# Half a batch of the last residual moved from transposes to GpSimd adds by channel, and the loads split by step

## The chip, the cores and the metric

One NeuronCore of a Trainium2 chip runs the whole program. The metric is device time in microseconds of one execution; lower is better. Engines are named as the profile names them: PE is TensorE, DVE is VectorE, ACT is ScalarE, POOL is GpSimd, SP is the engine whose queue issues nearly all DMAs.

## The reference

The input `x` has 4 batches of 128 channels and 64 × 64 positions, float32. Per batch three things follow each other:

```python
# layer 0: attention over all 4096 positions, 64 media channels, no mask
out = x + wo @ (softmax(k^T q) v)
# layer 1: LayerNorm per position, causal attention, 128 channels
t = t + attn(ln_t(t))
# feed-forward: LayerNorm, W, BatchNorm over all positions of all batches, then a recurrence
def step(yt, wx_t):
    yt = jax.nn.sigmoid(wx_t + yt @ Vt)
    return (yt, yt)
y0 = zeros;  _, ys = jax.lax.scan(step, y0, swapaxes(Wx, 0, 1))
t = t + swapaxes(ys, 0, 1)
```

The scan runs over 4096 positions of each batch. The result is returned by channel.

## The kernel before

`fast_path` does the work; `general_path` is a plain second form behind a branch, taken only if a flag says that the fast one's assumptions did not hold. It did not run in the profiled execution.

**Attention.** For each batch b come the blocks of layer 0 and then those of layer 1, in the order g = 1, 0, 2, ..., 7 (a block is 512 positions). A loop over slots issues scores, exponentials, sums and products; what follows a block is a chain of small steps, each pushed into a list with a due slot (`push`, `yield n, step`), at most one step of each layer being run in a slot. The chain of a block of layer 1 is `finish1`: `first` (line 886 on) divides and adds the residual into `xs`, and for batches from `BY_C` = 2 on stores the block by token into the DRAM tile `x2t` (line 898, four DMAs); `norm` and `second` prepare the input of the feed-forward; for the batches below `BY_C` a step `kept` (line 925) brings the block to channels first with one DVE transpose (`squares`, line 758) and stores it into the DRAM tile `x2c` (line 765, four DMAs); `third` writes the feed-forward's product W·x over the block in `xs`.

**Recurrence.** The scan is cut into `NCH` = 256 chunks of `STEPS` = 16 positions per batch. All chunks run side by side: each is warmed up for `WARM` = 6 steps on the positions before it, and then takes its 16 steps. So a step of one batch is one product of 128 × 256 columns. `step(b, s)`: PE multiplies the states by `vf` into `ps_y` (line 1317), DVE adds the scaled input (`z`, line 1328), ACT applies the sigmoid (line 1332). A round s runs the four batches, then `residual(s - 1)`, then `add(s)`. From s = 1 on the orders on PE, DVE, ACT, POOL and SP are pinned (`pin`) as written.

**Output.** Batches 0 and 1 leave by channel: `add(s)` adds the states of step s and `xc` (512 columns, line 1339) on GpSimd and stores the sum (line 1341). `sums` has three buffers. Batches 2 and 3 leave by token: `residual(s)` transposes four tiles of 128 × 128 states on PE (line 1348) into `ps_r`, DVE adds them to `xr` in place (line 1352), and SP stores that (line 1353).

**Loads.** `xc` (two DMAs of 2 MB from `x2c`, line 1272) and then `xr` (four of 1 MB from `x2t`, line 1277) are issued on SP in that order just behind the last stores of line 898. After the rounds the kernel compares end states with start states (`difference`, `away`, lines 1375 to 1389), forms the flag (line 1414), and all engines load it and branch.

Of the kernel before, what the change touches and what calls it, by code (L numbers as in the profile page):

```python
# [15 lines left out]
P = 128  # L16
# [5 lines left out]
BY_C = 2  # L22
# [4 lines left out]
def general_path(  # L27
# [12 lines left out]
    f_gamma: bass.AP,  # L40
    f_beta: bass.AP,
    out_c: bass.AP,
    out_t: bass.AP,
):
    nc = tc.nc
# [241 lines left out]
    with tc.tile_pool(name="wx", bufs=1) as wxp, tc.tile_pool(name="fwork", bufs=3) as wk:  # L287
        wx = wxp.tile([P, N, B], F32, name="wx")
        stats = wxp.tile([P, B * NB, nc.vector.BN_STATS_DIM], F32, name="stats")
        with tc.tile_pool(name="ps_ln", bufs=2, space=PSUM) as ps_ln, tc.tile_pool(  # L290
            name="ps_wx", bufs=3, space=PSUM
        ) as ps_wx:
            for b in range(B):

                def project(blk, xhat, b=b):
                    wp = ps_wx.tile([P, BLK], F32, tag="w", name="wx_ps")
                    nc.tensor.matmul(wp, lhsT=wf, rhs=xhat, start=True, stop=True)
                    nc.vector.bn_stats(stats[:, b * NB + blk, :], wp)
                    nc.scalar.copy(wx[:, ts(blk, BLK), b], wp)

                layernorm(b, ps_ln, wk, project)


        mv = wxp.tile([P, nc.vector.BN_AGGR_DIM], F32, name="mv")
        nc.vector.bn_aggr(mv, stats)
        scale = wxp.tile([P, 1], F32, name="scale")
        nc.vector.tensor_scalar(scale, mv[:, 1:2], BN_EPS, None, ALU.add)
        nc.vector.reciprocal(scale, scale)
        nc.scalar.activation(scale, scale, AF.Sqrt)
        nc.vector.tensor_tensor(scale, scale, gamma, ALU.mult)  # L310
        shift = wxp.tile([P, 1], F32, name="shift")
        nc.vector.tensor_tensor(shift, mv[:, 0:1], scale, ALU.mult)
        nc.vector.tensor_tensor(shift, beta, shift, ALU.subtract)

        STEPS = BLK // B
        with tc.tile_pool(name="ys", bufs=3) as ysp, tc.tile_pool(
            name="ps_y", bufs=2, space=PSUM
        ) as ps_y, tc.tile_pool(name="ps_o", bufs=2, space=PSUM) as ps_o:

            def preload(kb):  # L320
                wn = wk.tile([P, STEPS, B], F32, tag="wn", name="wn")
                nc.vector.tensor_scalar(wn, wx[:, ts(kb, STEPS), :], scale, shift, ALU.mult, ALU.add)
                ps = ps_y.tile([P, STEPS, B], F32, tag="y", name="y_ps")
                nc.tensor.matmul(ps, lhsT=ident, rhs=wn, start=True, stop=False, skip_group_check=True)
                return ps

            nblk = N // STEPS
            prev = None
            nxt = preload(0)
            for kb in range(nblk):  # L330
                ps = nxt
                y = ysp.tile([P, STEPS, B], F32, tag="y", name="y")
                for t in range(STEPS):
                    if prev is not None:
                        nc.tensor.matmul(
                            ps[:, t, :], lhsT=vf, rhs=prev, start=False, stop=t == STEPS - 1, skip_group_check=True
                        )
                    nc.scalar.activation(y[:, t, :], ps[:, t, :], AF.Sigmoid)
                    prev = y[:, t, :]
                    if t == STEPS // 2 and kb + 1 < nblk:  # L340
                        nxt = preload(kb + 1)
                o = ysp.tile([P, B, STEPS], F32, tag="o", name="o")
                nc.gpsimd.tensor_tensor(o, xs[:, :, ts(kb, STEPS)], y.rearrange("p t b -> p b t"), ALU.add)

                S = out_c.shape[2]
                K = STEPS // S
                g, j = kb // TPB, kb % TPB
                for b in range(BY_C):
                    oc = ysp.tile([P, S, K], F32, tag="oc", name="oc")
                    nc.vector.tensor_copy(oc, o[:, b].rearrange("p (k s) -> p s k", s=S))  # L350
                    for q in range(TPB):
                        nc.sync.dma_start(out=out_c[b, :, :, ds(((g * TPB + q) * TPB + j) * 2, 2)], in_=oc[:, :, ts(q, 2)])
                op = ps_o.tile([P, B - BY_C, P], F32, tag="o", name="oT_ps")
                for b in range(BY_C, B):
                    nc.tensor.transpose(op[:, b - BY_C, :], o[:, b, :], ident)
                oT = ysp.tile([P, B - BY_C, P], F32, tag="oT", name="oT")
                nc.vector.tensor_copy(oT, op)
                R = STEPS // TPB
                for q in range(TPB):
                    nc.sync.dma_start(  # L360
                        out=out_t[:, ds(((g * TPB + q) * TPB + j) * R, R), :].rearrange("b n c -> n b c"), in_=oT[ts(q, R)]
                    )

# [1 line left out]
def fast_path(  # L367
# [13 lines left out]
    f_gamma: bass.AP,  # L381
    f_beta: bass.AP,
    out_c: bass.AP,
    out_t: bass.AP,
    flag: bass.AP,
):
# [25 lines left out]
    xs = xpool.tile([P, B, N], F32, name="xs")  # L412


    x2c = dram.tile([BY_C, P, N], F32, name="x2c")
    x2t = dram.tile([B - BY_C, N, P], F32, name="x2t")

    joint = const.tile([P, 2 * B, P], F32, name="joint")
    slots = iter(range(2 * B))
# [97 lines left out]
    with tc.tile_pool(name="batch", bufs=1) as batch, tc.tile_pool(name="rows", bufs=2) as rowp, tc.tile_pool(  # L517
# [363 lines left out]
        def finish1(b, g, turn):  # L881
# [4 lines left out]
            def first():  # L886
                denominators(1, b, g, mem["own"])
                joined(1, b, g, mem["op"] if turn else projected1(agg, final))
                if final:
                    early_product(1, *WHOLE[0])  # L890
                    early_sigmoid(1, *WHOLE[0])
                    for part in WHOLE[1:]:
                        early_step(1, part)
                    early_step(2, WHOLE[0])
                if b >= BY_C:
                    to = x2t[b - BY_C, ts(g, BLK)].rearrange("(q j t) c -> q t j c", q=Q, j=TPB)
                    for q in range(Q):
                        nc.sync.dma_start(out=to[q], in_=xs[ts(q, S), b, ts(g, BLK)].rearrange("p (j c) -> p j c", c=P))
                mem["xh"] = wk.tile([P, TPB, P], F32, tag="xh2", name="xh2")
                mem["of"] = moments(b, g)  # L900
                if final:
                    in_range(True)
# [4 lines left out]
            def second():  # L907
# [10 lines left out]
                    return  # L918


                by_c = dram2.tile([P, BLK], F32, tag="by_c", name="by_c")
                stored(mem["xh"], by_c)
                nc.sync.dma_start(out=mem["xhT"], in_=by_c)

            def kept():

                stored(xs[:, b, ts(g, BLK)].rearrange("p (j c) -> p j c", c=P), x2c[b, :, ts(g, BLK)])

            def third():

# [46 lines left out]
            if not final:  # L977
                yield 1, norm
            yield 2, second
            if b < BY_C:  # L980
                yield 1, kept
            if turn:
                late.append(third)
# [278 lines left out]
    with tc.tile_pool(name="xr", bufs=1) as xrp, tc.tile_pool(name="y", bufs=2) as yp, tc.tile_pool(  # L1262
# [3 lines left out]
    ) as ps_r, tc.tile_pool(name="ps_m2", bufs=1, space=PSUM) as ps_m2, tc.tile_pool(name="ps_y", bufs=1, space=PSUM) as ps_y:  # L1266

        HALVES = NCH // P
        by_chunk = lambda t: t.rearrange("b n c -> (b n) c").rearrange("(m q s) c -> s q m c", q=P, s=STEPS)
        xc = xrp.tile([P, BY_C, NCH, STEPS], F32, name="xc")  # L1270
        for b in range(BY_C):
            pin(nc.sync.dma_start(out=xc[:, b].rearrange("p k s -> p (k s)"), in_=x2c[b]))
        xr = xrp.tile([P, B - BY_C, HALVES, STEPS, P], F32, name="xr")
        for b in range(B - BY_C):
            for h in range(HALVES):
                pin(
                    nc.sync.dma_start(
                        out=xr[:, b, h], in_=x2t[b].rearrange("(h q s) c -> h q s c", q=P, s=STEPS)[h]
                    )
                )  # L1280

        mv = xrp.tile([P, nc.vector.BN_AGGR_DIM], F32, name="mv")
        nc.vector.bn_aggr(mv, ends)
# [50 lines left out]

        def add(s):

            t = sums.tile([P, BY_C, NCH], F32, tag="sum", name="sum")
            by_grid = lambda t: t.rearrange("p b (g c) -> p b g c", c=CPB)
            ins = nc.gpsimd.tensor_tensor(by_grid(t), by_step[:, :BY_C, s], by_grid(xc[:, :, :, s]), ALU.add)
            tc.keep_in_program_order(ins)  # L1340
            tc.keep_in_program_order(nc.sync.dma_start(out=out_c[:, :, s].rearrange("b c k -> c b k"), in_=t))


        def residual(s):

            ps = ps_r.tile([P, TPB, P], F32, tag="r", name="yT_ps")
            for j in range(TPB):
                ins = nc.tensor.transpose(ps[:, j], states(BY_C + j // HALVES, s)[:, j % HALVES], ident)
                if not j:
                    pin(ins)  # L1350
            t = xr.rearrange("p b h s c -> p (b h) s c")[:, :, s]
            pin(nc.vector.tensor_tensor(t, t, ps, ALU.add))  # L1352
            pin(nc.sync.dma_start(out=by_chunk(out_t)[s], in_=t))

        met = ps_m2.tile([P, BY_C, NCH], F32, name="met")
        gap = xrp.tile([P, B], F32, name="gap")
# [124 lines left out]
```

## Time and profile before

| what | us |
|---|---|
| median of three runs (2014.79 to 2014.90) | 2014.89 |
| the profiled execution | 2014.68 |
| its span, first to last instruction | 2012.9 |
| last scores of the attention start | 1941.96 |
| first `x2c` load issued (line 1272) | 1951.62 |
| first step of the recurrence with the final scale (line 1328) | 1957.87 |
| first `add` on GpSimd (line 1339) | 1971.67 |
| first matmul of the comparison (line 1375) | 2005.44 |
| flag written (line 1414) | 2009.16 |

Some 1950 us are attention, and some 50 us the recurrence; the rest is the end. In the page a busy share is over the whole span, so the engines of the last 55 us have to be looked at by themselves. DMA issues of the page that matter here:

```profile
x2c<-sqT SPq DMA_DIRECT2D x64, 64.0 KB, 1.8
x2t<-xs SPq DMA_DIRECT2D x64, 64.0 KB, 1.8
...
xc<-x2c SPq DMA_DIRECT2D x2, 2048.0 KB, 10.1
xr<-x2t SPq DMA_DIRECT2D x4, 1024.0 KB, 17.4
out_x<-sum SPq DMA_DIRECT2D x16, 256.0 KB, 2.2
out_x<-xr SPq DMA_DIRECT2D x16, 256.0 KB, 2.3
```

The last column is the median time in us from the issue to the landing. A start with a duration in a timeline merges neighbouring instructions of one kind ("x4"); what stands in brackets is the idle time of the engine ahead of it and what ended it.

### The profile page before, as it was taken

How to read it: one execution, taken by the hardware profiler on the slowest of the kernel's cores; microseconds unless marked ns; L12 is line 12 of the kernel's file. 1: busy time of each engine (PE TensorE's matmuls, PEld its weight loads, DVE VectorE, ACT ScalarE, POOL GpSimd, SP SyncE). 2: the span in 40 equal slices, each digit the busy share in tenths (PEclk: the TensorE clock that was granted, in tenths of full speed). 3: DMA queues.
4: the chain of work that ended last, by engine and by line, in shares of the span. 5: the costliest groups of instructions: out<-in, count | busy, mean ns of one | idle time of the engine just before them, and what ended most of it. 6: DMA issues, size and time to landing. Idle time of an engine off the chain costs nothing.

```text
span 2012.9 us, 31340 instructions
## 1 busy us (share of the span) xinstructions
PE 2003.2 (100%) x11896; PEld 875.4 (43%) x11896; DVE 1456.0 (72%) x2816; ACT 974.7 (48%) x1053; POOL 140.3 (7%) x241
## 2 busy tenths in 40 slices
PE   9999999999999999999999999999999999999998
PEld 3333354444333345444433334444433333544457
DVE  4799877545789987555589997654478998764568
ACT  5666633332666653333466664333356665333247
POOL 1000011000000001000000001000000000110014
PEclk9999999999999999999999999999999999999999
DMA  3111112210110111320111111231010111120027
GB/s 106 44 34 23 22 33 59 63 43 16 43 54 14 22 23 40 72 69 16 43 34 47 23 23 28 53 79 37 16 43 2 23 22 23 32 53 17 16 99 257
DMA packets 218603, 89.02 MB, mean 44 GB/s; under 512 B 142176, under 2 KB 203360, under 8 KB 217680
## 3 DMA queue, kind: packets, MB, share of 16 engines
q1 hardware_dynamic: 217728, 86.43, 17.4%
q8 instruction: 94, 1.54, 0.3%
q14 instruction: 61, 0.50, 0.1%
q0 software_dynamic: 288, 0.39, 0.1%
q10 hardware_dynamic: 432, 0.16, 0.0%
HBM read 45.84 MB, written 36.89 MB: 41 GB/s over the span
## 4 chain that ended last, share of the span: by engine, by line
PE 96%; DVE 2%; DMA 1%; ACT 0%; issue 0%; SPq 0%; POOL 0%; DVEq 0%; ACTq 0%; POOLq 0%
PE s_ps L1034 23%; PE acc L1094 22%; PE acc L1083 22%; PE s_ps L1019 22%; PE o_ps L688 1%; PE r_ps L639 1%; PE wx_ps L956 1%; PE kr_ps L576 1%; DVE z L1328 1%; DMA xr<-x2t 1%; PE v_ps L588 1%; PE o_ps L700 1%; DVE xr L1352 0%; ACT p L1028 0%; PE warm_ps L533 0%
## 5 line engine op out<-in xcount | busy, mean ns | idle before, releaser
L1063 DVE TENSOR_TENSOR dsum<-dsum,p 128x1024 f32<-128x1024 f32 x692 | 845.3, 1222 | 402.5 <-ACT p L1037 295.7
L1028 ACT ACTIVATE p<-s_ps,nshift 128x1024 f32<-128x1024 f32 x512 | 570.0, 1117 | 312.6 <-PE s_ps L1019 286.8
L1037 ACT ACTIVATE p<-s_ps 128x1024 f32<-128x1024 f32 (+2 forms) x288 | 274.5, 953 | 601.8 <-PE s_ps L1034 580.0
L1083 PE MATMUL acc<-p,v 64*64 64x512 f32 x4096 | 527.9, 589 | 0.0
L1019 PE MATMUL s_ps<-kr,swap 64*64 64x512 f32 x2048 | 522.6, 590 | 1.3 <-ACT p L1028 1.3
L1019 PE MATMUL s_ps<-kr 64*64 64x512 f32 x2048 | 522.6, 590 | 0.0
L1034 PE MATMUL s_ps<-rows,xhT 128*128 128x512 f32 (+3 forms) x1152 | 500.7, 558 | 0.0
L1094 PE MATMUL acc<-p,xh 128*128 128x512 f32 (+3 forms) x1152 | 500.2, 557 | 0.0
L1034 PEld LDWEIGHTS s_ps<-rows,xhT 128*128 128x128 f32 x1152 | 215.0, 190 | 244.7 <-issue 202.7
L1094 PEld LDWEIGHTS acc<-p,xh 128*128 128x128 f32 x1152 | 216.1, 190 | 239.8 <-issue 223.4
L1083 PEld LDWEIGHTS acc<-p,v 64*64 64x64 f32 x4096 | 156.6, 133 | 282.9 <-issue 274.3
L1019 PEld LDWEIGHTS s_ps<-kr,swap 64*64 64x64 f32 x2048 | 141.7, 133 | 144.6 <-issue 135.7
L1019 PEld LDWEIGHTS s_ps<-kr 64*64 64x64 f32 x2048 | 141.7, 133 | 134.6 <-issue 133.1
L728 POOL TENSOR_TENSOR ln_rstd<-ln_var,mhalf 128x4 f32<-128x4 f32 x64 | 69.9, 1093 | 1185.5 <-DVE ln_var L726 1185.4
L1071 DVE TENSOR_TENSOR dsum<-dsum,p 128x256 f32<-128x256 f32 (+1 forms) x120 | 56.0, 499 | 59.8 <-POOL p L1043 59.8
L714 DVE SCALAR_TENSOR_TENSOR xs<-o_ps,recs,xs 128x128 f32<-128x128 f32 x256 | 70.5, 343 | 5.4 <-PE o_ps L700 1.7
L744 DVE TENSOR_SCALAR xh<-xs,ln_mv,ln_rstd 128x128 f32<-128x128 f32 x252 | 70.1, 341 | 1.9
L723 DVE BATCH_NORM_STATS2 ln_st<-xs 128x6 f32<-128x128 f32 x256 | 62.8, 271 | 0.0
L1043 POOL TENSOR_SCALAR_AFFINE_SELECT p<-p 128x128 f32<-128x128 f32 x128 | 34.5, 293 | 352.3 <-ACT p L1037 348.0
L1061 DVE COPY dsum<-p 128x1024 f32<-128x1024 f32 x44 | 30.2, 686 | 24.6 <-ACT p L1037 15.3
L758 DVE STREAM_TRANSPOSE sqT<-xh 128x512 f32<-128x512 f32 x63 | 44.6, 709 | 1.7
L961 ACT COPY xs<-wx_ps 128x512 f32<-128x512 f32 x31 | 18.1, 585 | 50.2 <-DVE stats L957 46.4
(170 smaller groups left out, 892.7 us busy)
## 6 DMA issues: line engine op xcount, KB each, us to landing
xs<-in_xT SPq DMA_DIRECT2D x32, 256.0 KB, 3.1
by_r<-sqT SPq DMA_DIRECT2D x128, 64.0 KB, 2.2
xhT<-by_r SPq DMA_DIRECT2D x128, 64.0 KB, 2.0
by_c<-sqT SPq DMA_DIRECT2D x124, 64.0 KB, 1.8
xhT<-by_c SPq DMA_DIRECT2D x31, 256.0 KB, 2.8
xs<-in_x SPq DMA_DIRECT2D x12, 512.0 KB, 5.5
swap<-kr SPq DMA_DIRECT2D x32, 128.0 KB, 2.3
x2c<-sqT SPq DMA_DIRECT2D x64, 64.0 KB, 1.8
```

The lines of the kernel that those rows point to most:

```text
L714: nc.vector.scalar_tensor_tensor(t, in0=op[:, ts(j, P)], scalar=rec[:, j : j + 1], in1=t, op0=ALU.mult, op1=ALU.add)
L723: nc.vector.bn_stats(st[:, j], xs[:, b, ds(g * BLK + j * P, P)])
L728: nc.gpsimd.tensor_tensor(y, var, mhalf, ALU.pow)
L744: nc.vector.tensor_scalar(dst[:, j], xs[:, b, ds(g * BLK + j * P, P)], mv[:, j, 0:1], y[:, j : j + 1], ALU.subtract, ALU.mult)
L1019: ins = nc.tensor.matmul(ps[c * M : c * M + M, ts(r, BLK)], lhsT=keys[:, ts(c, M)], rhs=rows[r], start=True, stop=True,)
L1028: nc.scalar.activation(it.p, ps, AF.Exp, bias=nshift)
L1034: nc.tensor.matmul(ps[:, off : off + n], lhsT=lhsT, rhs=rhs, start=True, stop=True)
L1037: ins = nc.scalar.activation(it.p[:, :off], ps[:, :off], AF.Exp, scale=float(P) ** -0.5)
L1063: nc.vector.tensor_tensor(flat, flat, it.p, ALU.add)
L1071: nc.vector.tensor_tensor(den[:, h, q0:], den[:, h, q0:], it.p[:, o : o + n], ALU.add)
L1083: ins = nc.tensor.matmul(bt.acc[c * M : c * M + M, r], lhsT=bt.v[part, m * TPB + j, h], rhs=it.p[part, ts(c, BLK)], start=it.first, stop=i ...
L1094: ins = nc.tensor.matmul(bt.acc[:, 0, q0:], lhsT=bt.xh[:, t], rhs=it.p[:, o : o + n], start=it.first and h == 0, stop=it.last and h == 1,)
```

## The change

The first half of batch 2 (positions 0 to 2047) changes sides: in the attention its four blocks are kept by channel in `x2c` rather than by token in `x2t`, and in the rounds GpSimd adds its 128 columns in a second instruction with a store of its own. `residual` is left with three tiles (`UNITS`): the second half of batch 2 and both halves of batch 3. The loads of `xr` are split by step: the first four of the sixteen steps are loaded ahead of `xc`, the rest after it and the new `xh`.

```diff
+    by_c = lambda b, g: b < BY_C or b == BY_C and g < NB // 2
...
-                if b >= BY_C:
-                    to = x2t[b - BY_C, ts(g, BLK)].rearrange("(q j t) c -> q t j c", q=Q, j=TPB)
+                if not by_c(b, g):
+                    to = x2t[ds((b - BY_C) * N - N // 2 + g * BLK, BLK)].rearrange("(q j t) c -> q t j c", q=Q, j=TPB)
...
-            if b < BY_C:
+            if by_c(b, g):
                 yield 1, kept
...
+        UNITS = (B - BY_C) * HALVES - 1
+        by_chunk = lambda t: t.rearrange("(m q s) c -> q m s c", q=P, s=STEPS)
         xc = xrp.tile([P, BY_C, NCH, STEPS], F32, name="xc")
+        xh = xrp.tile([P, P, STEPS], F32, name="xh")
+        xr = xrp.tile([P, UNITS, STEPS, P], F32, name="xr")
+
+        def load_by_token(part):
+            for m in range(UNITS):
+                pin(nc.sync.dma_start(out=xr[:, m, part], in_=by_chunk(x2t)[:, m, part]))
+
+        load_by_token(slice(0, STEPS // 4))
         for b in range(BY_C):
-            pin(nc.sync.dma_start(out=xc[:, b].rearrange("p k s -> p (k s)"), in_=x2c[b]))
-        xr = xrp.tile([P, B - BY_C, HALVES, STEPS, P], F32, name="xr")
-        for b in range(B - BY_C):
-            for h in range(HALVES):
-                pin(
-                    nc.sync.dma_start(
-                        out=xr[:, b, h], in_=x2t[b].rearrange("(h q s) c -> h q s c", q=P, s=STEPS)[h]
-                    )
-                )
+            pin(nc.sync.dma_start(out=xc[:, b].rearrange("p k s -> p (k s)"), in_=x2c[:, ts(b, N)]))
+        pin(nc.sync.dma_start(out=xh.rearrange("p k s -> p (k s)"), in_=x2c[:, ds(BY_C * N, N // 2)]))
+        load_by_token(slice(STEPS // 4, STEPS))
...
-            t = sums.tile([P, BY_C, NCH], F32, tag="sum", name="sum")
+            t = sums.tile([P, BY_C * NCH + P], F32, tag="sum", name="sum")
+            whole, half = t[:, : BY_C * NCH].rearrange("p (b c) -> p b c", b=BY_C), t[:, BY_C * NCH :]
             by_grid = lambda t: t.rearrange("p b (g c) -> p b g c", c=CPB)
-            ins = nc.gpsimd.tensor_tensor(by_grid(t), by_step[:, :BY_C, s], by_grid(xc[:, :, :, s]), ALU.add)
-            tc.keep_in_program_order(ins)
-            tc.keep_in_program_order(nc.sync.dma_start(out=out_c[:, :, s].rearrange("b c k -> c b k"), in_=t))
+            pin(nc.gpsimd.tensor_tensor(by_grid(whole), by_step[:, :BY_C, s], by_grid(xc[:, :, :, s]), ALU.add))
+            pin(nc.sync.dma_start(out=out_c[:, :, s].rearrange("b c k -> c b k"), in_=whole))
+            pin(nc.gpsimd.tensor_tensor(half, states(BY_C, s)[:, 0], xh[:, :, s], ALU.add))
+            pin(nc.sync.dma_start(out=out_h[:, s], in_=half))
...
-            ps = ps_r.tile([P, TPB, P], F32, tag="r", name="yT_ps")
-            for j in range(TPB):
-                ins = nc.tensor.transpose(ps[:, j], states(BY_C + j // HALVES, s)[:, j % HALVES], ident)
+            ps = ps_r.tile([P, UNITS, P], F32, tag="r", name="yT_ps")
+            for j in range(UNITS):
+                b, h = BY_C + (j + 1) // HALVES, (j + 1) % HALVES
+                ins = nc.tensor.transpose(ps[:, j], states(b, s)[:, h], ident)
...
-            t = xr.rearrange("p b h s c -> p (b h) s c")[:, :, s]
+            t = xr[:, :, s]
             pin(nc.vector.tensor_tensor(t, t, ps, ALU.add))
-            pin(nc.sync.dma_start(out=by_chunk(out_t)[s], in_=t))
+            pin(nc.sync.dma_start(out=by_chunk(out_t)[:, :, s], in_=t))
```

`x2c` and `x2t` become DRAM tiles of two dimensions with that half batch in the former; `general_path` and the host's reordering of the output follow suit.

More of the change, by code (lines that the diff above doesn't have):

```diff
@@ L42, in general_path @@
     out_c: bass.AP,
+    out_h: bass.AP,
     out_t: bass.AP,
@@ L347, in general_path @@
                 g, j = kb // TPB, kb % TPB
-                for b in range(BY_C):
+                chans = BY_C + (g < NB // 2)
+                for b in range(chans):
                     oc = ysp.tile([P, S, K], F32, tag="oc", name="oc")
                     nc.vector.tensor_copy(oc, o[:, b].rearrange("p (k s) -> p s k", s=S))
+                    to = out_c[b] if b < BY_C else out_h
                     for q in range(TPB):
-                        nc.sync.dma_start(out=out_c[b, :, :, ds(((g * TPB + q) * TPB + j) * 2, 2)], in_=oc[:, :, ts(q, 2)])
+                        nc.sync.dma_start(out=to[:, :, ds(((g * TPB + q) * TPB + j) * 2, 2)], in_=oc[:, :, ts(q, 2)])
                 op = ps_o.tile([P, B - BY_C, P], F32, tag="o", name="oT_ps")
-                for b in range(BY_C, B):
+                for b in range(chans, B):
                     nc.tensor.transpose(op[:, b - BY_C, :], o[:, b, :], ident)
                 oT = ysp.tile([P, B - BY_C, P], F32, tag="oT", name="oT")
-                nc.vector.tensor_copy(oT, op)
+                nc.vector.tensor_copy(oT[:, chans - BY_C :], op[:, chans - BY_C :])
                 R = STEPS // TPB
-                for q in range(TPB):
-                    nc.sync.dma_start(
-                        out=out_t[:, ds(((g * TPB + q) * TPB + j) * R, R), :].rearrange("b n c -> n b c"), in_=oT[ts(q, R)]
-                    )
+                for b in range(chans, B):
+                    for q in range(TPB):
+                        row = (b - BY_C) * N - N // 2 + ((g * TPB + q) * TPB + j) * R
+                        nc.sync.dma_start(out=out_t[ds(row, R)], in_=oT[ts(q, R), b - BY_C])
 @with_exitstack
@@ L383, in fast_path @@
     out_c: bass.AP,
+    out_h: bass.AP,
     out_t: bass.AP,
@@ L412, in fast_path @@
     xs = xpool.tile([P, B, N], F32, name="xs")
-    x2c = dram.tile([BY_C, P, N], F32, name="x2c")
-    x2t = dram.tile([B - BY_C, N, P], F32, name="x2t")
+    x2c = dram.tile([P, BY_C * N + N // 2], F32, name="x2c")
+    x2t = dram.tile([(B - BY_C) * N - N // 2, P], F32, name="x2t")
+    by_c = lambda b, g: b < BY_C or b == BY_C and g < NB // 2
     joint = const.tile([P, 2 * B, P], F32, name="joint")
@@ L918, in second @@
                     return
-                by_c = dram2.tile([P, BLK], F32, tag="by_c", name="by_c")
-                stored(mem["xh"], by_c)
-                nc.sync.dma_start(out=mem["xhT"], in_=by_c)
+                chans = dram2.tile([P, BLK], F32, tag="chans", name="chans")
+                stored(mem["xh"], chans)
+                nc.sync.dma_start(out=mem["xhT"], in_=chans)
             def kept():
-                stored(xs[:, b, ts(g, BLK)].rearrange("p (j c) -> p j c", c=P), x2c[b, :, ts(g, BLK)])
+                stored(xs[:, b, ts(g, BLK)].rearrange("p (j c) -> p j c", c=P), x2c[:, ds(b * N + g * BLK, BLK)])
             def third():
@@ L1268, in fast_path @@
         HALVES = NCH // P
-        by_chunk = lambda t: t.rearrange("b n c -> (b n) c").rearrange("(m q s) c -> s q m c", q=P, s=STEPS)
+        UNITS = (B - BY_C) * HALVES - 1
+        by_chunk = lambda t: t.rearrange("(m q s) c -> q m s c", q=P, s=STEPS)
         xc = xrp.tile([P, BY_C, NCH, STEPS], F32, name="xc")
-        for b in range(BY_C):
-            pin(nc.sync.dma_start(out=xc[:, b].rearrange("p k s -> p (k s)"), in_=x2c[b]))
-        xr = xrp.tile([P, B - BY_C, HALVES, STEPS, P], F32, name="xr")
-        for b in range(B - BY_C):
-            for h in range(HALVES):
-                pin(
-                    nc.sync.dma_start(
-                        out=xr[:, b, h], in_=x2t[b].rearrange("(h q s) c -> h q s c", q=P, s=STEPS)[h]
-                    )
-                )
+        xh = xrp.tile([P, P, STEPS], F32, name="xh")
[4 more added lines that the diff above has]
+        load_by_token(slice(0, STEPS // 4))
+        for b in range(BY_C):
+            pin(nc.sync.dma_start(out=xc[:, b].rearrange("p k s -> p (k s)"), in_=x2c[:, ts(b, N)]))
+        pin(nc.sync.dma_start(out=xh.rearrange("p k s -> p (k s)"), in_=x2c[:, ds(BY_C * N, N // 2)]))
+        load_by_token(slice(STEPS // 4, STEPS))
         mv = xrp.tile([P, nc.vector.BN_AGGR_DIM], F32, name="mv")
@@ L1463 @@
     k = h * w // STEPS
-    y = [y[:BY_C].rearrange("b (c s k) -> b c s k", s=STEPS, k=k), y[BY_C:].rearrange("b (n c) -> b n c", c=c)]
+    half = c * h * w // 2
+    y = [
+        y[:BY_C].rearrange("b (c s k) -> b c s k", s=STEPS, k=k),
+        y[BY_C, :half].rearrange("(c s k) -> c s k", s=STEPS, k=k // 2),
+        y.rearrange("b (h n c) -> (b h) n c", h=2, c=c)[2 * BY_C + 1 :].rearrange("u n c -> (u n) c"),
+    ]
     both = [ins["in_c_wqkT"], ins["in_c_wkqT"]]
@@ L1477, with by_channel, by_token @@
     y = np.asarray(r.results[0]["out_x"])
-    y_c = y[:BY_C].reshape(-1, c, STEPS, k // 32, 4, 4, 2).transpose(0, 1, 3, 5, 4, 6, 2).reshape(-1, c, h, w)
-    y_t = y[BY_C:].reshape(-1, k // 32, 4, 4, 2 * STEPS, c).transpose(0, 5, 1, 3, 2, 4).reshape(-1, c, h, w)
-    return np.concatenate([y_c, y_t])
+    y = y.reshape(2 * b, half)
+    def by_channel(t):
+        t = t.reshape(-1, c, STEPS, k // 64, 4, 4, 2).transpose(0, 1, 3, 5, 4, 6, 2)
+        return t.reshape(-1, c, h * w // 2)
+    def by_token(t):
+        return t.reshape(-1, k // 64, 4, 4, 2 * STEPS, c).transpose(0, 5, 1, 3, 2, 4).reshape(-1, c, h * w // 2)
+    y_c = y[: 2 * BY_C].reshape(-1, c, STEPS, k // 32, 4, 4, 2).transpose(0, 1, 3, 5, 4, 6, 2).reshape(-1, c, h * w)
+    y_h = np.concatenate([by_channel(y[2 * BY_C]), by_token(y[2 * BY_C + 1 :])])
+    y_t = y_h.reshape(-1, 2, c, h * w // 2).transpose(0, 2, 1, 3).reshape(-1, c, h * w)
+    return np.concatenate([y_c, y_t]).reshape(b, c, h, w)
```

## The prediction

> **What bounds the kernel now.** I read the page first (busy shares and chain), then the table of windows over the last 60 us, then the timelines of PE, DVE, GpSimd and SP there.
>
> ```profile
> PE 2003.2 (100%) x11896; PEld 875.4 (43%) x11896; DVE 1456.0 (72%) x2816; ACT 974.7 (48%) x1053; POOL 140.3 (7%) x241
> PE 96%; DVE 2%; DMA 1%; ACT 0%; issue 0%; SPq 0%; POOL 0%; DVEq 0%; ACTq 0%; POOLq 0%
> ```
>
> 96% of the chain is PE. All that the change does before 1950 us lies in the attention of batch 2, where PE is the chain; what it does after that lies in the recurrence. There the average share of 72% for DVE is of no use; the windows are:
>
> ```profile
> 1970.00:1980.00 10.00, 9.57 (x60) 8.25 (x60) 7.92 (x19) 6.99 (x17) 4.76 (x4) 1.00 0.64 231
> 1980.00:1990.00 10.00, 10.00 (x57) 8.49 (x56) 10.00 (x24) 8.24 (x21) 7.48 (x5) 1.00 0.77 243
> 1990.00:2000.00 10.00, 10.00 (x58) 8.62 (x56) 10.00 (x24) 8.14 (x20) 6.87 (x6) 1.00 0.80 248
> ```
>
> The columns are length, then PE, PEld, DVE, ACT and POOL busy, granted clock, DMA share, GB/s. In the rounds PE and DVE are both full. One round in the timelines of these two:
>
> ```profile
> 1998.94 1.89 PE L1317 MATMUL y_ps<-xs,vf 128*128 128x256 f32 x8
> 2000.67 0.60 PE L1348 MATMUL yT_ps<-ident,xs 128*128 128x128 f32 x4
> 2001.11 1.89 PE L1317 MATMUL y_ps<-xs,vf 128*128 128x256 f32 x8
> ...
> 1999.93 1.64 DVE L1328 SCALAR_TENSOR_TENSOR z<-xs,all_scale,y_ps 128x256 f32<-128x256 f32 x4
> 2001.50 0.67 DVE L1352 TENSOR_TENSOR xr<-xr,yT_ps 128x512 f32<-128x512 f32 x1
> 2002.10 1.64 DVE L1328 SCALAR_TENSOR_TENSOR z<-xs,all_scale,y_ps 128x256 f32<-128x256 f32 x4
> ```
>
> Start to start, PE spends 1.73 us on the four steps and 0.44 on four transposes (0.109 each): 2.17. DVE spends 1.57 on four z (0.392 each) and 0.60 on the residual: 2.17. Between transposes(1) at 1979.01 and transposes(14) at 2005.00 there are 12 rounds of 2.166 us. So a gain needs both engines lighter; the change takes from both.
>
> At the start of the rounds there is one stall. Line 1352 needs all four loads of `xr`, and the last of them takes 21 us:
>
> ```profile
> 1975.51 0.69 DVE L1352 TENSOR_TENSOR xr<-xr,yT_ps 128x512 f32<-128x512 f32 x1 [0.85 <-PE y_ps L1317]
> ...
> 1977.18 1.13 PE L1317 MATMUL y_ps<-xs,vf 128*128 128x256 f32 x4 [0.43 <-ACT xs L1332]
> ...
> 1954.10 21.19 DMA xr<-x2t
> ```
>
> The first line names PE as releaser, but that matmul was long done; 1954.10 plus 21.19 is 1975.29, just ahead of the 1975.51, so it was the load. The z of the next round queue behind it. Transposes(0) and (2) are 1973.98 and 1979.01, 5.03 apart where two rounds are 4.33: the stall costs 0.70 us.
>
> GpSimd has room, but not much:
>
> ```profile
> 2001.47 1.54 POOL L1339 TENSOR_TENSOR sum<-xs,xc 128x512 f32<-128x512 f32 x1 [0.64 <-ACT xs L1332]
> 2003.63 1.53 POOL L1339 TENSOR_TENSOR sum<-xs,xc 128x512 f32<-128x512 f32 x1 [0.62 <-ACT xs L1332]
> ```
>
> 1.53 us of 2.17 busy, then 0.63 idle until the next states exist.
>
> **What the Trainium skill says.** (1) GPSIMD Engine Reference, Elementwise: about 2.6 cycles per element for a two-input `tensor_tensor`, and 4497 ns measured for 2048 fp32 columns. This trace has 1534 ns for 512, 3.0 ns a column, dearer than the page's 2.2; here one operand is read with a step of 64 bytes. (2) SBUF — State Buffer, Who interferes with whom: a DVE instruction with two SBUF inputs and a GpSimd instruction that reads SBUF block each other. The trace agrees in the attention: the copy of line 1173 (4 columns) takes 1117 ns beside `dsum<-dsum,p` (1217 ns) and ends 50 ns after it. In the rounds z and the residual read one input from PSUM, and the adds are 1523 to 1554 ns all along, so I expect no blocking. (3) Perfetto Trace Analysis, GPSIMD Engine Instruction: durations there do not compose; use start to start. The trace agrees: two `affine_select` of 292 ns together fill 540, so they start some 250 apart.
>
> **The change, part by part.**
> *Batch 2 in the attention, blocks 0 to 3.* Four stores of line 898 per block leave `first`; `kept` comes a slot later, with one DVE transpose (709 ns, row L758) and four stores (0.45 us of SP each, as line 898's). Four blocks: 2.8 us of DVE in some 260 us of which DVE is busy 155. This is what batch 1 does in all its eight blocks. Layer 1 of batch 1, from the chain, runs from 725.68 to 985.91 (260.23 us), and of batch 2, without `kept`, from 1210.39 to 1470.71 (260.32). Cost: 0, bounds −0.1 and +0.1; PE covers it. Nothing reads `x2c` before 1951 us.
>
> *Loads.* First the steps 0 to 3 of three units (0.79 MB), then `xc` (4.19), `xh` (1.05), then the rest of `xr` (2.36): the same 8.39 MB, at the 410 to 440 GB/s of the trace some 20 us. Nine issues for six, at 0.45 us each, and the third quarter must wait for the last stores of `x2t` (issued until 1951.5, 1.8 us to landing), with `xc` behind it on SP. I give this 0.5 to 1 us. Residual(0) then has its data by 1956. `xc` and `xh` are there after 6.03 MB, at 1968 to 1969; add(0) needs them at 1971.67 as before (2.5 us of slack). The rest comes by 1976.5; residual(4) needs it at 1983. So the stall of 0.70 goes, and what is late next is PE itself.
>
> *PE.* One transpose less: 2.166 − 0.109 = 2.057 us a round.
> *DVE.* 384 columns for 512. The row of `dsum` has 0.69 for 512 and 1.22 for 1024, about 1.04 ns a column: −0.133, so 2.033 a round. DVE stays just under PE. The way round one batch (matmul, z, sigmoid, matmul) takes 1.81 us in the warm-up rounds of the timeline, below 2.057, so it does not take over.
>
> Sum: the rounds begin at transposes(0), 1973.98, as before; 14 periods of 2.057 and three transposes end at 2003.11 where line 1375 starts now at 2005.44: −2.33. That is 0.70 of stall, 14 × 0.109 = 1.53, and 0.11 in the last transposes. The tail behind it (difference, last residual, flag) has one more transpose and one more short residual in line: about −0.13. Flag from 2009.16 to 2006.7; span 2012.9 − 2.46 = 2010.4, if nothing else is last.
>
> *GpSimd.* Its round gets a second add of 128 columns, not shown in the trace. Below: strictly by columns, 128/512 of 1534 = 384 ns, some 0.43 with a start. From other two-input operations of this trace: `pow` takes 547 ns for 1 column and 1006 for 4, so a fixed part up to 0.39, leaving 2.23 ns a column: 0.68. Above: a line through 1534 and the skill's 4497 has 0.55 fixed and 1.93 a column: 0.79. Start to start is 0.05 less each. I take 0.55: 1.49 + 0.50 = 1.99 us a round, 0.07 under PE. Range 1.87 to 2.23, or 2.33 with no overlap. At my value add(15) starts at about 2003.4, ends at 2005.4; its two stores and the last residual's go out by 2006.4 and land 2.3 us later, 2008.7. SP's waits at the end run now from 2010.6 to 2012.0, so then from 2008.2 to 2009.5: it may cost 0 to 0.3. I take 0.1. The adds wait for states that ACT has written and for a `sums` buffer of three rounds ago, whose store (2.2 us) landed by then. Behind add(15) on GpSimd only its load of the flag is queued; on SP, the last residual's store.
> *SP.* Three stores of 0.37 a round for two: 1.1 of 2.06. Bytes are the same.
>
> Sum in all: −2.35. Profiled execution: span 2010.55 against 2012.9; it took 2014.68, 1.78 more than its span, and the median of the three runs, 2014.89, is 0.21 above that. Forecast for the median: **2012.5**.
>
> **Rivals.**
> A, the above: 2012.0 to 2012.9. Chance 0.52.
> B, GpSimd takes the round over by a little (2.08 to 2.2 us). add(2) starts at 1976.6 and the adds end at 1976.6 + 14 × period: 2006.5 at 2.13, and the last store lands 2.85 us later, at 2009.3, with up to a microsecond of SP's waits behind it. 2012.8 to 2014.3. For it: the `pow` fixed part. Chance 0.20.
> C, slower: the same place, but the second add costs a whole instruction, 0.79 with no overlap, 2.33 us a round. Adds end at 2009.2, the last landing is 2012.1, and behind it come 0.95 (its wait the last of SP's row) to 2.27 us (the first): span 2013.0 to 2014.3, median about 2015.7. It decides from a period of 2.22 to 2.32. For it: the skill's two-point line. Against: `affine_select` of 128 columns takes 0.29. Chance 0.11.
> D, the split load frees nothing: residual(0) is made to wait for every load of `xr`, now ending at 1976.5 rather than 1975.3. The stall is then 0.7 to 1.9 and the gain 1.7 to 0.5: 2013.2 to 2014.4. Against: the store of one step's columns does not hold the next residual now, so parts of the tile are told apart. Chance 0.06.
> E, something I do not see (the order of unpinned work, memory places of the new tiles): either sign, 0.11.
>
> **How the numbers follow.** 0.2% is 4.03 us; about that can be told from no change. A to D are all inside it. Only E goes beyond: faster 0.05, slower 0.06, rest within. The range 2011.9 to 2015.0 takes A, B, D and a part of C and E; the likeliest case alone is 2012.0 to 2012.9.
>
> **What would show it.** PE: transposes 2.057 us apart, no idle at the third round. DVE: residual 0.54 us, starting right after transposes(0). GpSimd: adds start 2.06 apart and the pair fills 1.99 of it; if the starts are further apart and the idle gap is gone, B or C. Loads: first quarter landed by 1956, the rest after 1975. Layer 1 of batch 2: 260.3 us again. The forecast fails if the second add takes over 0.6 us, or if batch 2 shifts.

## The result, and the profile after

| | before | after |
|---|---|---|
| median, us (22 runs each) | 2015.06 | 2012.38 |
| from to | 2014.48 to 2016.03 | 2011.93 to 2013.42 |
| profiled execution, us | 2014.68 | 2012.34 |
| its span | 2012.9 | 2010.6 |

The ratio is 0.9987 (0.9981 to 0.9993): a gain of 0.13%, inside the 0.2% of the forecast "no change", and with an interval that leaves out 1. The forecast was 2012.5.

Four stretches of time show where the 2.24 us of the span went (2012.87 to 2010.63). Each figure is a difference of two times in one trace:

| stretch, us | before | after | change | forecast |
|---|---|---|---|---|
| start to transposes(0) | 1973.98 | 1974.26 | +0.28 | 0 |
| transposes(0) to the first matmul of the comparison | 31.46 | 29.12 | −2.34 | −2.33 |
| comparison to flag | 3.72 | 3.51 | −0.21 | −0.13 |
| flag to end | 3.71 | 3.74 | +0.03 | +0.1 |

The +0.28 need not come from the change. The kernel after is 0.35 late already when the first product of batch 1 starts (501.55 for 501.20 in the chain), long before batch 2. And kernels with the same attention scatter by more: transposes(0) start at 1973.98 in the kernel before, and at 1975.00, 1974.83 and 1974.30 in runs 1, 7 and 8 below, which leave its attention as it is. Layer 1 of batch 2, which now keeps four blocks by channel, takes 1210.74 to 1470.98, 260.24 us (before 260.32): PE covers the four DVE transposes and their stores.

From the page of after, the shares of the chain and the busy times:

```profile
PE 99%; ACT 0%; DVE 0%; issue 0%; POOL 0%; DVEq 0%; ACTq 0%; POOLq 0%
...
PE 2001.4 (100%) x11880; PEld 874.8 (44%) x11880; DVE 1456.4 (72%) x2820; ACT 974.7 (48%) x1053; POOL 147.3 (7%) x257
```

The 2% of DVE and the 1% of DMA, the load of `xr`, are gone from the chain. PE has 16 instructions fewer than before and POOL 16 more, one for each round; the four more of DVE are the transposes of `kept`. The windows of after (columns as before: length, PE, PEld, DVE, ACT, POOL, clock, DMA share, GB/s):

```profile
1970.00:1980.00 10.00, 10.00 (x64) 8.94 (x62) 8.77 (x21) 7.79 (x18) 7.13 (x7) 1.00 0.88 318
1980.00:1990.00 10.00, 10.00 (x55) 8.77 (x54) 10.00 (x25) 9.04 (x22) 9.86 (x11) 1.00 0.81 250
1990.00:2000.00 10.00, 10.00 (x56) 8.75 (x55) 10.00 (x25) 8.38 (x20) 9.57 (x11) 1.00 0.82 250
```

PE is full in the first window too, where it had 9.57. POOL went from 7.48 to 9.86 of 10: the change has used up nearly all its room. One round of PE and of DVE after, from their timelines:

```profile
1997.21 1.89 PE L1325 MATMUL y_ps<-xs,vf 128*128 128x256 f32 x8
1998.94 0.49 PE L1359 MATMUL yT_ps<-ident,xs 128*128 128x128 f32 x3
1999.27 1.89 PE L1325 MATMUL y_ps<-xs,vf 128*128 128x256 f32 x8
```

```profile
1997.95 1.68 DVE L1336 SCALAR_TENSOR_TENSOR z<-xs,all_scale,y_ps 128x256 f32<-128x256 f32 x4
1999.54 0.55 DVE L1363 TENSOR_TENSOR xr<-xr,yT_ps 128x384 f32<-128x384 f32 x1
2000.01 1.67 DVE L1336 SCALAR_TENSOR_TENSOR z<-xs,all_scale,y_ps 128x256 f32<-128x256 f32 x4
```

From 1997.21 to 1999.27 are 2.06 us where there were 2.17, and the residual of 0.55 us starts 0.60 us after the first of its transposes. DVE looks full on both sides (1.68 and 0.55, with no idle time shown between them); whether it has room left can't be read here, which is what one experiment is for. GpSimd after, in a stretch where it catches up after one late start:

```profile
1995.69 1.54 POOL L1348 TENSOR_TENSOR sum<-xs,xc 128x512 f32<-128x512 f32 x1 [0.36 <-ACT xs L1340]
1997.19 0.52 POOL L1350 TENSOR_TENSOR sum<-xs,xh 128x128 f32<-128x128 f32 x1
1997.68 1.53 POOL L1348 TENSOR_TENSOR sum<-xs,xc 128x512 f32<-128x512 f32 x1
```

The three lines follow each other without a wait, so the starts give GpSimd's own period: 1995.69 to 1997.68 is 1.99 us. The two durations would add up to 2.06, PE's round, and would read as no room at all. This is the reading by starts that the Trainium skill asks for (Perfetto Trace Analysis, GPSIMD Engine Instruction), and the trace agrees.

### The profile page after: what moved, and what is told of

Its sections match the earlier page's. It is cut to its first block, busy times and chain, and to the rows that moved or that the text cites. A ratio compares the mean times of both kernels' runs of the same rounds, so it can differ in the third digit from the quotient of the medians.

```text
span 2010.6 us, 31386 instructions
## 1 busy us (share of the span) xinstructions
PE 2001.4 (100%) x11880; PEld 874.8 (44%) x11880; DVE 1456.4 (72%) x2820; ACT 974.7 (48%) x1053; POOL 147.3 (7%) x257
## 4 chain that ended last, share of the span: by engine, by line
PE 99%; ACT 0%; DVE 0%; issue 0%; POOL 0%; DVEq 0%; ACTq 0%; POOLq 0%
PE s_ps L1039 23%; PE acc L1099 22%; PE acc L1088 22%; PE s_ps L1024 22%; PE y_ps L1325 2%; PE o_ps L693 1%; PE r_ps L644 1%; PE wx_ps L961 1%; PE kr_ps L581 1%; PE v_ps L593 1%; PE o_ps L705 1%; ACT p L1033 0%; PE yT_ps L1359 0%; PE warm_ps L538 0%; PE y_ps L1334 0%; PE early_ps L818 0%
## 5 line engine op out<-in xcount | busy, mean ns | idle before, releaser
L657 DVE TENSOR_REDUCE part<-sq 128x16 f32<-128x512 f32 x64 | 41.6, 671 | 0.8
```

## The experiments

The theory, T: the gain in the rounds is made of two separate things, a stall of 0.70 us at their start that the split loads take away, and a shorter period, which PE sets; DVE and GpSimd come just below it. Rivals: the period is set by DVE; or by GpSimd; or the loads matter only together with the columns. "Round" below is the period, and "stretch" is transposes(0) to the first matmul of the comparison.

**1. The loads alone.** The kernel before, with the loads of `xr` split:

```diff
+        load_by_token(slice(0, STEPS // 4))
         for b in range(BY_C):
             pin(nc.sync.dma_start(out=xc[:, b].rearrange("p k s -> p (k s)"), in_=x2c[b]))
...
+        load_by_token(slice(STEPS // 4, STEPS))
```

> The kernel before, with the loads of xr split by step (first quarter ahead of xc) and nothing else changed: four transposes, 512 columns. If the stall of the third round is the load of xr (my theory), residual(0) starts right after its transposes, PE has no idle gap in the third round, transposes(0) to transposes(2) are 4.33 us apart instead of 5.03, rounds stay at 2.166, and from transposes(0) to the first comparison it is 30.76 us instead of 31.46: about 0.70 us faster as a whole. If the split frees nothing (rival D), it stays 31.46 or more.

Measured: in the rounds what T expects, a period of 2.166 from the first round on. The third round has no idle time on PE, where the kernel before had 0.43:

```profile
1977.16 0.60 PE L1350 MATMUL yT_ps<-ident,early 128*128 128x128 f32 x4
1977.60 1.03 PE L1319 MATMUL y_ps<-xs,vf 128*128 128x256 f32 x4
```

The stretch is 30.76, 0.70 shorter. But the median is 2016.64 beside 2015.26, a ratio of 1.0007 (0.9999 to 1.0016): the total misses the expectation. Flag to end takes 6.21 us in place of 3.71. In the trace SP stops for 2.40 us, from 2012.14 to 2014.56, in the row of instructions behind the branch, and all other engines wait for it there. Runs 7 and 8 follow this up.

**2. The columns alone.** The kernel after, with whole loads of `xr` at the end:

```diff
-        load_by_token(slice(0, STEPS // 4))
...
-        load_by_token(slice(STEPS // 4, STEPS))
+        load_by_token(slice(0, STEPS))
```

> The changed kernel with the loads in the order of before: xc, xh, then xr whole. My theory: rounds of 2.057 us, but the stall is back; residual(0) waits until about 1975.4 to 1976, and since DVE has only 0.024 us a round to catch up, nearly all of it stays: transposes(0) to the first comparison 29.8 to 30.4 us against 29.12 in the changed kernel, 0.7 to 1.2 us slower than that one. Rival: with a lighter DVE the stall is absorbed, 29.1 to 29.3.

Measured: 2013.38, ratio 0.999 (0.9982 to 0.9999); the stretch is 29.88, and one round of 2.813 among those of 2.057. The residual(0) on DVE, and PE a round later, from the two timelines:

```profile
1976.38 0.56 DVE L1362 TENSOR_TENSOR xr<-xr,yT_ps 128x384 f32<-128x384 f32 x1 [0.81 <-DMA xr<-x2t]
```

```profile
1977.92 1.13 PE L1324 MATMUL y_ps<-xs,vf 128*128 128x256 f32 x4 [0.49 <-ACT xs L1339]
```

The stall is there again, and here the bracket names the load itself. It costs 0.76, as before it had cost 0.70: the loads' part stands on its own.

**3. PE's part taken back.** The kernel after, with a fourth transpose on PE that DVE does not read:

```diff
-            for j in range(UNITS):
+            for j in range(-1, UNITS):
...
-            pin(nc.vector.tensor_tensor(t, t, ps, ALU.add))
+            pin(nc.vector.tensor_tensor(t, t, ps[:, 1:], ALU.add))
```

> The changed kernel with the fourth transpose put back on PE, its result not used; DVE still adds 384 columns. If PE sets the round (theory), 2.166 us a round and DVE idle by some 0.13 in each, transposes(0) to the first comparison 30.7 us. If DVE set the round before and PE only kept step with it (rival), it stays near 2.06 and 29.1.

Measured: 2014.41, ratio 0.9995 (0.9986 to 1.0003), the stretch 30.76. From PE's timeline:

```profile
1996.54 0.60 PE L1359 MATMUL yT_ps<-ident,xs 128*128 128x128 f32 x4
1996.98 1.89 PE L1325 MATMUL y_ps<-xs,vf 128*128 128x256 f32 x8
1998.71 0.60 PE L1359 MATMUL yT_ps<-ident,xs 128*128 128x128 f32 x4
```

2.17 again, while DVE and GpSimd do the same work as in the kernel after. One transpose on PE takes back the whole 1.64 us that the columns had given (29.12 to 30.76): PE sets the round.

**4. How much room DVE has.** The kernel after, with one more DVE operation in a round. It has 128 columns, as many as the residual had lost, but as an operation of its own:

```diff
+            extra = yp.tile([P, P], F32, tag="extra", name="extra")
+            pin(nc.vector.tensor_tensor(extra, ident, ps[:, 0], ALU.add))
```

> The changed kernel with one more DVE instruction a round (128 columns, read from PSUM and from a constant, result not used), some 0.19 us start to start by the rows of 128 columns. If DVE stands 0.024 us under PE (theory), DVE takes the round over at 2.033 + 0.19 = 2.22 us, transposes(0) to the first comparison about 31.5. If DVE has more room than its full windows show (rival), the rounds stay at 2.06 to 2.1.

Measured: 2014.88, ratio 0.9999 (0.9991 to 1.0008), the stretch 31.32. From DVE's timeline:

```profile
1996.92 0.58 DVE L1363 TENSOR_TENSOR xr<-xr,yT_ps 128x384 f32<-128x384 f32 x1
1997.39 0.31 DVE L1365 TENSOR_TENSOR extra<-ident,yT_ps 128x128 f32<-128x128 f32 x1
1997.59 1.68 DVE L1336 SCALAR_TENSOR_TENSOR z<-xs,all_scale,y_ps 128x256 f32<-128x256 f32 x4
1999.15 0.58 DVE L1363 TENSOR_TENSOR xr<-xr,yT_ps 128x384 f32<-128x384 f32 x1
```

The round is 2.23, and the extra operation takes 0.20 of it from start to start (1997.39 to 1997.59). Without it DVE's own period is 2.03, 0.02 to 0.03 below PE's. By this sum a residual of 512 columns (0.60 in place of 0.47) would have held the round at 2.16, and PE's lighter round would have brought next to nothing; no run has tried that.

**5. GpSimd made the bound.** The second add over 256 columns, of which half is thrown away:

```diff
+            twice = xh[:, :, s].unsqueeze(1).to_broadcast([P, HALVES, P])
+            pin(nc.gpsimd.tensor_tensor(pair(half), states(BY_C, s), twice, ALU.add))
+            pin(nc.sync.dma_start(out=out_h[:, s], in_=half[:, :P]))
```

> The changed kernel with the second GpSimd add over 256 columns instead of 128 (both halves of batch 2, the second result not stored), PE and DVE as in the changed kernel. From its two adds (534 and some 1534 ns for 128 and 512) a line gives 0.86 us for 256, so 1.49 + 0.82 = 2.31 us a GpSimd round against 2.057 on PE. If the round of PE and DVE does not hang on GpSimd (theory), transposes stay 2.057 apart and the comparison starts as in the changed kernel, but the adds end at about 2009 instead of 2005.6 and the last stores land some 2.9 us later: 2 to 4 us slower than the changed kernel, at or over the time of before (rival C's place). If the end absorbs late adds, it is within 1 us of the changed kernel.

Measured: 2015.5 beside 2015.12, ratio 1.0002 (0.9993 to 1.001): the whole gain is gone. The rounds of PE are untouched (2.057, stretch 29.12), while GpSimd needs 2.31 (adds at 1979.15 and 1981.46). What the late adds hold up is seen on DVE, in `count`, the operation that compares the differences with their tolerances for the flag. It is shown for the kernel after, and then for run 5 with the last adds:

```profile
2006.25 0.16 DVE L1419 TENSOR_TENSOR count<-gap,tol 128x4 f32<-128x4 f32 x1 [0.15 <-ACT sq L1393]
```

```profile
2006.15 3.08 DVE L1420 TENSOR_TENSOR count<-gap,tol 128x4 f32<-128x4 f32 x1 [0.16 <-ACT sq L1394]
```

```profile
2006.03 0.90 POOL L1351 TENSOR_TENSOR sum<-xs,xh 128x256 f32<-128x256 f32 x1
2006.83 1.57 POOL L1348 TENSOR_TENSOR sum<-xs,xc 128x512 f32<-128x512 f32 x1
2008.31 0.91 POOL L1351 TENSOR_TENSOR sum<-xs,xh 128x256 f32<-128x256 f32 x1
```

`count`, four columns with two operands in SBUF, takes 3.08 us (0.16 in the kernel after) and ends at 2009.23, when the last add does (2009.22). The flag comes at 2009.71 in place of 2006.89, and the end with it (flag to end 3.90, in the kernel after 3.74). The Trainium skill describes such a lock between a DVE instruction with two inputs in SBUF and a GpSimd instruction that reads SBUF (SBUF — State Buffer, Who interferes with whom). `count` fits it, with one difference: it lasted through three adds in a row, not only the one that was under way. The two operations `d` of the same trace (end states less start states) don't fit: they too have both operands in SBUF and ran beside adds, from 2004.02 on, and took 0.74 us together. So that a lock is the cause is not shown; that `count` ended only with the last add is.

**6. What a column costs GpSimd.** The kernel after, with the second operand of both adds read from neighbouring columns. These are the wrong positions, so the sums are of no use; how many columns are added stays the same:

```diff
-            pin(nc.gpsimd.tensor_tensor(by_grid(whole), by_step[:, :BY_C, s], by_grid(xc[:, :, :, s]), ALU.add))
+            pin(nc.gpsimd.tensor_tensor(by_grid(whole), by_step[:, :BY_C, s], by_grid(xc.rearrange("p b k s -> p b (k s)")[:, :, ts(s, NCH)]), ALU.add))
...
-            pin(nc.gpsimd.tensor_tensor(half, states(BY_C, s)[:, 0], xh[:, :, s], ALU.add))
+            pin(nc.gpsimd.tensor_tensor(half, states(BY_C, s)[:, 0], xh.rearrange("p k s -> p (k s)")[:, ts(s, P)], ALU.add))
```

> The changed kernel with the second operand of both GpSimd adds read from neighbouring columns of xc and xh instead of with a step of 16 (which positions are added changes, not how many). If the step makes a column dearer (by the skill's 2.2 ns a column), 512 columns take 1.1 to 1.2 us and 128 some 0.35 to 0.45, GpSimd has 0.5 us to spare, and the time is that of the changed kernel since PE sets the round. If the step costs nothing (rival), 1.53 and 0.53 again.

Measured: 2012.23, ratio 0.9986 (0.9979 to 0.9992), the time of the kernel after, since PE sets the round. From POOL's timeline:

```profile
1995.77 1.30 POOL L1348 TENSOR_TENSOR sum<-xs,xc 128x512 f32<-128x512 f32 x1 [0.65 <-ACT xs L1340]
1997.02 0.47 POOL L1350 TENSOR_TENSOR sum<-xs,xh 128x128 f32<-128x128 f32 x1
```

A line through the medians of the two adds (1.290 and 0.469) has 2.14 ns a column ((1.290 − 0.469) / 384) and 0.20 us fixed. With the step of 64 bytes it is 2.64 ns and 0.18 us ((1.534 − 0.520) / 384, from the medians in the kernel after). The Trainium skill's 4497 ns for 2048 columns (GPSIMD Engine Reference, Elementwise) is 2.2 a column and agrees with the first; it is the step that makes the adds of this kernel dearer.

**7 and 8. The gap of run 1.** As in run 1, with the rest of `xr` in fewer or in more DMAs. Neither edits anything near the end; they shift how many instructions SP has run by then.

```diff
# run 7: two DMAs for the rest
+            pin(nc.sync.dma_start(out=xr[:, b, :, STEPS // 4 :], in_=src[:, :, STEPS // 4 :]))
# run 8: parts of two steps
+        for k in range(STEPS // 4, STEPS, 2):
+            load_by_token(slice(k, k + 2))
```

> The loads-only kernel (e1) with the rest of xr in two DMAs instead of four: the same data in the same order, two issues fewer on SP. e1 lost 2.4 us in one gap of SP after the branch, behind its row of semaphore waits, where neither the kernel before nor the changed one has a gap. If that gap comes from where SP's last instructions lie in its stream (theory), two fewer move it: flag to end is back at 3.7 us from 6.2, and the kernel is 0.5 to 0.8 us faster than before. If it comes from the split loads themselves (rival), flag to end stays at about 6.2 and the kernel 1.4 slower than before.

> The loads-only kernel (e1) with the rest of xr in parts of two steps: 28 issues on SP instead of 8, the same data. In e1 and e7 the gap on SP behind the branch comes at the same place of SP's stream, behind its 1495th instruction in the records (e1: 20 after the branch, e7: 23). Here SP has about 24 instructions more than e1, so that place lies ahead of the branch, in the rounds. If the gap is a fetch of SP's next instructions that is hidden when it falls in the rounds (theory), flag to end is 3.7 us, from transposes(0) to the comparison it is 30.76 again, and the kernel is 0.4 to 0.9 us faster than before. If split loads cost the end something (rival), flag to end is over 5.

| kernel | place of the branch among SP's recorded instructions | gap behind the 1496th, us | flag to end, us | median, us | before, us |
|---|---|---|---|---|---|
| run 1 | 1476th | 2.40 | 6.21 | 2016.64 | 2015.26 |
| run 7 | 1473rd | 1.92 | 5.28 | 2015.77 | 2015.12 |
| run 8 | 1496th | 0.45 | 3.70 | 2014.6 | 2015.32 |

The table counts from 1; the expectation of run 8 counts from 0 and has 1495 for the same place. The ratios of 7 and 8 are 1.0003 (0.9995 to 1.0011) and 0.9996 (0.9987 to 1.0004); the stretch is 30.76 in both.

The expectation of run 7, no gap, missed; but the gap stayed at the same number, counted from the program's start, while the branch moved by three. Run 8 has 20 instructions more than run 1, where about 24 were expected, so the place falls on the branch itself and not in the rounds. There SP stands for 0.45 us, as behind the branch of run 1 (0.44), and the gap is gone. Flag to end is back at 3.70, though the loads are in still more parts, so split loads as such don't cost it. The median lies 0.7 us under the kernel before, as much as the loads are worth, but the interval of the ratio takes in 1.

The kernel before ends at its 1493rd instruction and never reaches the place. The kernel after passes it in the rounds, 12 instructions ahead of its branch, and shows no such gap. That SP waits there for its instructions to be fetched is a guess from the place and not shown: the trace of run 1 records five packets of instruction queues from 2009.6 to 2012, but no packet at all from 2012.1 to 2014.5.

**9. A layout that a strided read likes.** Run 6 reads the wrong columns; the same speed needs neighbours in memory. `x2c` is laid out so that eight neighbouring chunks of one step lie side by side. The DVE transpose of `kept` writes that order, and GpSimd reads it:

```diff
-        xc = xrp.tile([P, BY_C, NCH, STEPS], F32, name="xc")
+        xc = xrp.tile([P, BY_C, NCH // E, STEPS, E], F32, name="xc")
...
+                    out=sq.rearrange("p c s j u -> p c j u s"),
```

> The changed kernel with x2c laid out so that eight neighbouring columns of one step lie side by side: only the output pattern of the DVE transpose in kept changes, and how xc and xh are read. If GpSimd pays for the step of 64 bytes (theory, from the run with neighbouring columns: 1.30 and 0.47 us), its two adds take about 1.3 and 0.47 us here too, and the time is that of the changed kernel, PE setting the round. If runs of eight don't help (rival), 1.53 and 0.53. The transposes of kept may take longer than 709 ns; PE covers them.

Measured: 2012.48, ratio 0.9986 (0.9979 to 0.9992). The adds take 1287 and 468 ns in the median, as with neighbours throughout (1290 and 469). The 20 transposes take 1088 ns for 698, and PE hides that.

**10. The room used.** Run 9 with all of batch 2 by channel: GpSimd 768 columns, PE two transposes, DVE a residual of 256 columns.

```diff
-    by_c = lambda b, g: b < BY_C or b == BY_C and g < NB // 2
+    by_c = lambda b, g: b <= BY_C
...
-        UNITS = (B - BY_C) * HALVES - 1
+        UNITS = (B - BY_C) * HALVES - 2
```

> As the runs-of-eight kernel, with all of batch 2 by channel: GpSimd adds 768 columns, PE has two transposes, DVE adds 256 columns. PE 1.73 + 0.22 = 1.95 us a round, DVE 1.57 + 0.33 = 1.90, GpSimd 1.24 + 0.69 = 1.93 (2.16 ns a column and 0.19 fixed, from the run with neighbouring columns). If PE still sets the round, transposes(0) to the comparison 27.5 us against 29.12, and the kernel is 1.6 us faster than the changed one, 4.3 faster than before. If GpSimd takes over (rival), its adds end late and the gain on the changed kernel is under 1 us.

Measured: 2010.84 (2010.53 to 2011.79) beside 2015.32, ratio 0.9978 (0.9969 to 0.9987), and 1.64 under run 9 of the same series. It is faster than both kernels: none of its times reaches the lowest of the kernel before (2014.41 in this series) or after (2011.93). The stretch is 27.48. From POOL's timeline and from the windows:

```profile
1996.63 1.28 POOL L1359 TENSOR_TENSOR sum<-xs,xc 128x512 f32<-128x512 f32 x1
1997.88 0.74 POOL L1370 TENSOR_TENSOR sum<-xs,xh 128x256 f32<-128x256 f32 x1
1998.58 1.28 POOL L1359 TENSOR_TENSOR sum<-xs,xc 128x512 f32<-128x512 f32 x1
```

```profile
1980.00:1990.00 10.00, 10.00 (x53) 8.63 (x52) 10.00 (x27) 9.36 (x24) 10.00 (x11) 1.00 0.85 273
```

GpSimd's period is 1.95 (1996.63 to 1998.58), and PE's is 1.948 (2.057 less one transpose): GpSimd is full and has no more to give. Its first add from `xh` waits 1.24 us for the load of `xh`, now twice as large, and this is hardly made up. The adds end at 2004.45, 0.28 ahead of `count` (2004.73).

## Why the prediction was right

- **The stall, −0.70.** Alone it brings 0.70 in the rounds (run 1), and without it 0.76 are lost (run 2).
- **The period, 14 × 0.109 and 0.11.** Predicted 2.057, measured 2.057. (The 12 rounds from which 2.166 was read begin at transposes(2), not at transposes(1) as the prediction has it; the sum is right.) Runs 1 and 3 split the 2.34 of the stretch into 0.70 for the loads (31.46 to 30.76) and 1.64 for the columns (30.76 to 29.12), the two terms of the sum.
- **DVE at 2.033.** It worked out to 2.03 (run 4). The step that DVE stays just under PE held by 0.02 to 0.03.
- **GpSimd at 1.99.** The second add was taken at 0.55 and takes 0.52 in the stretch shown; the period is 1.99. That 0.55 was a choice inside wide bounds, since no row showed a small add. Both higher bounds had too large a fixed part: up to 0.39 by way of `pow`, and 0.55 by a line that joined this kernel's strided add with the Trainium skill's large one, whose cost a column is that of neighbouring columns in run 6. The adds measured have 0.18 to 0.20 (run 6).
- **`kept` at 0.** Layer 1 of batch 2 is 260.24.
- **The loads.** The first quarter is there by 1956.8 (said: 1956) and the rest by 1976.5, as said. `xh` lands at 1970.8, later than the 1968 to 1969 of the sum; this cost nothing, since its first add starts at 1973.4, but in run 10 it is what GpSimd waits for.
- **Tail and end.** The tail gave 0.21 where 0.13 was said: two residuals on DVE lie behind the start of the comparison (2005.83 and 2007.09 in the kernel before), not one, and each is 0.13 lighter; 0.21 of these 0.26 came through. The 0.1 for a late landing was not needed (flag to end +0.03). The start's +0.28 works against these, so that the sum's 2010.55 meets a measured 2010.6 is partly this cancelling. That 2012.5 meets 2012.38 is partly luck as well: the median of the kernel before moves from 2014.89 to 2015.32 between series.
- **Rival C** had the place right and the mechanism wrong. A GpSimd period of 2.31 does cost all the gain (run 5: 2015.5, with 2015.7 forecast for 2.33), but not by the landing of the last store: `count` on DVE ends with the last add. In the kernel after, the last add ends at 2005.62 and `count` starts at 2006.25, so by this reading 0.63 us of lateness were free. The prediction had looked only at the store; it had ruled out blocking for the rounds, and did not look at the comparison behind them.

Run 1 shows a risk that the prediction did not see: the same edit of the loads, in a kernel that is otherwise the old one, costs 2.5 us at the end. The kernel after shows no such gap; that it escapes by its count of SP's instructions is the likely reason, and not shown.

## What to carry to other kernels

Where several engines are full in a round, take work from all of them, and find each one's own period first: by starts of instructions that follow each other without a wait, or by adding a small known cost and seeing whether the round grows. Split a big load by when its parts are needed. Judge an edit of less than a microsecond by the stretch it touches as well as by the total, since something at the far end, as in run 1, can hide it; and where an engine becomes late, look at what runs beside its last instructions, and not only at who waits for its result.

## What the runs showed of the hardware

- SP stopped for 2.40 and 1.92 us behind its 1496th recorded instruction where the branch was the 1476th and the 1473rd (runs 1, 7). Where the branch itself was the 1496th (run 8), or the place lay 12 instructions ahead of it (the kernel after), there was no such stop. The cause was not measured.
- DVE's `count` took 3.08 us, through three GpSimd adds, where it took 0.16 with no add beside it (run 5, the kernel after). Yet `d`, two operations of 256 columns, with both operands in SBUF as well, took 0.74 us together beside running adds in the same trace, as they do in the kernel after (0.75). What sets the two apart stays open.
- With one operand at a step of 64 bytes an add on GpSimd took 2.64 ns a column (the kernel after), with neighbouring columns 2.14 (run 6). Runs of eight values (32 bytes) were as fast as neighbours throughout: 1287 ns for 512 columns in run 9, 1290 in run 6.
- A DVE transpose of 128 × 512 took 1088 ns for 698 where its output is scattered in steps of eight values (run 9).
